# Two-layer attention with a recurrence: a projection one unit later, a later second load, and a reordered end

## The chip, the cores and the metric

The kernel runs on one core of a Trainium2 chip. The metric is the device time in microseconds (us), a median over runs. The engines are named as the profile names them: PE is TensorE, DVE is VectorE, ACT is ScalarE, POOL is GpSimd, SP is SyncE, which here only issues DMA transfers.

## The reference

The input is x of shape (4, 128, 64, 64), all fp32. Every image is taken as N = 4096 tokens of 128 channels. Layer 0 adds a full attention, layer 1 a causal one and then a recurrence:

```
x = x + conv_attention(groupnorm(x))     # q, k: 64 rows, v: 128; softmax over all 4096 keys
t = tokens(x)
t = t + causal_attention(layernorm(t))   # Wq, Wk, Wv: 128 x 128, scale 1/sqrt(128)
wx = batchnorm(layernorm(t) @ W)         # mean and variance over all 4 x 4096 tokens
y[k] = sigmoid(wx[k] + y[k-1] @ V.T)     # over the 4096 tokens of each image, y[-1] = 0
t = t + y
```

## The kernel before

**Units of attention.** For each image (batch b), each layer and each tile of QT = 512 queries (c from 0 to 7), the work is cut into units of two key blocks of 128. In layer 0 a tile has 16 units; in layer 1 it has only those up to the diagonal. A long loop over all units issues the scores of unit i (L1083 in layer 1, L1090 in layer 0), lets background work advance one step, and then issues the product of unit i-1 (L1134, which accumulates `av`). ScalarE turns scores into exponentials `s` (L1092, L1096), of which three buffers exist. VectorE adds them up in `total` (L1131).

**Background work.** It is written as generators. `step` advances every generator in `ends`, and the first ready one in `todo`, once for each unit. A `yield` in such a generator is thus a delay of one unit. The generators that matter here are:

- `gn_stats(b)`: statistics of image b by 8 `bn_stats` (L649), put in the list at the start of tile c = 2 of image 0 for the second image. They wait for the load of that image.
- `keys0(b, c)`: normalised tokens xg (L681), B0v added to X by POOL (L683), queries and keys pk (L686), the split of K into a high part (L707, L711) and a low part (L708), and the values pv (L715). For image 0 they are made during the first tile, one chunk of 512 keys (two units) after the other, as they are needed; those of the later images are made during layer 1 of the image before.
- `finish` (L942 to L966): the softmax sums, their reciprocals, and o = av / sum (L966).
- `project` (L971 to L985): in layer 1, it waits for some units, multiplies o by the value weights (po, L981), and adds the result to the residual as X2 (L984). The number of units waited for comes from the last line of `finish`.

A list scheduler then orders the instructions inside each engine, by its own costs and by what is ready. It may move an instruction far from its place in the program. Two stretches are kept in the order written: the first keys, and everything from `last_part` to `ordered.close()`.

**The loads of X.** `load_x(b)` issues 8 transfers of 256 KB on SP's queue (L508). With a second argument, POOL first copies a few columns of that argument over the target (L505), so that the transfers can't start before it. The second image is loaded this way, from `product` of unit 4 of the first tile.

**The last part.** The last tile is split in LAST = 384 queries and 128 queries. For the first 384, the product with the recurrence's weights is done early (`pw_early`), and only waits for their scales, which three matmuls spread over the partitions as a row (L917). ScalarE copies the row (L932), VectorE multiplies (L881, in `write_last`) and takes batch-norm statistics (L886). The same is done for the last 128 queries at the end (`raw_last`, L940). `scale` then merges all statistics to the gain and the bias of the batch norm.

**The recurrence.** The 4096 steps of an image are cut in chunks of CHUNK = (16, 16, 32, 32) steps, which all run side by side, each after WARM = 10 warm-up steps. Images 0, 1 and the pair (2, 3) form three chains. `first_step` is the first warm-up step, one sigmoid (L594), and for nearly all columns it uses a guessed scale before the true statistics are in. For the 15 columns of the last image that need the last queries (`BEHIND`), it is done afterwards with the true scale. `seed` puts gain times wx in PSUM (L1218), `advance` adds a matmul (L1233) and takes the sigmoid (L1234). Meanwhile VectorE adds finished steps to the residual (`residual`, L1258), in an order given by the list `late` with (image, first step, number of steps): 4 steps of a 32-step chunk are 512 elements a partition, 8 are 1024. When an image is complete, `store` sends its two halves (L1263). A check of the chunk boundaries (L1315 to L1328) follows, and its verdict decides on a branch to a slower general version.

Of the kernel before, what the change touches and what calls it, by code (L numbers as in the profile page):

```python
# [25 lines left out]
F32 = mybir.dt.float32  # L26
# [5 lines left out]
P = 128  # L32
QT = 512
# [431 lines left out]
CHUNK = (16, 16, 32, 32)  # L465
# [5 lines left out]
LAST = 384  # L471
# [3 lines left out]
def fast_kernel(  # L475
# [9 lines left out]
    nc = tc.nc  # L485
# [85 lines left out]
    def idle(ps, n):  # L571

        for _ in range(n):
            nc.tensor.matmul(ps, lhsT=nil, rhs=nil.unsqueeze(1).to_broadcast([P, QT // P, P]), start=True, stop=True)
# [14 lines left out]
    def first_step(b, at, n, scales):  # L589

        gain, bias = scales
        l = CHUNK[b] - WARM
        src = WX[b][:, l // 2, ds(at, n), l % 2]
        nc.scalar.activation(first[b][:, ds(at + 1, n)], src, AF.Sigmoid, scale=gain, bias=bias)  # L594

    with ExitStack() as actx:
# [10 lines left out]
        def misc(name):  # L607
            return ps_m.tile([P, QT], F32, tag="m", name=name)
# [269 lines left out]
        def write_last(off, w, row, pw):  # L878

            part = WX[B - 1][:, :, ds((N - QT + off) // CHUNK[-1], w // CHUNK[-1]), :]  # L880
            nc.vector.tensor_tensor(  # L881
                part.rearrange("p l s t -> p s l t"),
                *[t.rearrange("p (s l t) -> p s l t", l=CHUNK[-1] // 2, t=2) for t in (row, pw)], ALU.mult,
            )
            k = 9 if off else 3
            nc.vector.bn_stats(groups[:, k : k + 6], part)  # L886

        def last_part(av, pz, s):


            w, cols = P, ds(N - P, P)
            xt = X[B - 1][:, cols]
            wide = [ps_pair.tile([P, 2, QT], F32, tag="pair", name=f"last_{k}") for k in range(2)]
            avs = tmp.tile([P, QT], F32, tag="a", name="avs")[:, :w]
            nc.vector.tensor_copy(avs, av[:, :w])

            nc.scalar.activation(small.tile([P, 1], F32, name="sig"), s[:, 1, w - 1 : w], AF.Sigmoid)
            for b in range(2):
                first_step(b, 0, NC[b] - 1, scales["guess"])
            rz = small.tile([P, 1], F32, name="rz")  # L900
            nc.vector.reciprocal(rz, pz[:, 0:1])
            idle(misc("idle_last0"), 1)
            ptok = wide[0][:, 0, :w]
            nc.tensor.matmul(ptok, lhsT=avs, rhs=W1v, start=True, stop=True)
            prz = wide[1][:, 0, :w]
            nc.tensor.matmul(prz, lhsT=rz.to_broadcast([P, P]), rhs=ident, start=True, stop=True)
            po = misc("po_last")[:, :w]
            nc.tensor.matmul(po, lhsT=W1v, rhs=avs, start=True, stop=True)
            tok = scales["tok"]
            nc.vector.scalar_tensor_tensor(tok, ptok, rz, tok, ALU.mult, ALU.add)  # L910
            rzs = tmp.tile([P, QT], F32, tag="b", name="rzs")[:, :w]
            nc.scalar.copy(rzs, prz)

            pw_early, rstd_early = scales["early"]
            row = wide[1][:, 1, :LAST]
            for j in range(LAST // P):
                nc.tensor.matmul(  # L917
                    row[:, ts(j, P)], lhsT=rstd_early[:, j : j + 1].to_broadcast([P, P]), rhs=ident, start=True, stop=True
                )
            for b in range(2, B):  # L920
                first_step(b, 0, NC[b] - 1 - (BEHIND if b == B - 1 else 0), scales["guess"])
            stats = small.tile([P, 6], F32, name="lst_last")
            mv = small.tile([P, 2], F32, name="lmv_last")
            nc.vector.bn_stats(stats, tok)
            nc.vector.bn_aggr(mv, stats)
            rstd = small.tile([P, 1], F32, name="rstd_last")
            rsqrt(rstd, mv[:, 1:2], 1e-5, 1)
            nc.vector.scalar_tensor_tensor(rzs, rzs, GUARD, po, ALU.mult, ALU.mult)
            x2 = X2[B - 1][:, cols]
            nc.vector.scalar_tensor_tensor(x2, rzs, 1.0 / GUARD, xt, ALU.mult, ALU.add)  # L930
            rows = tmp.tile([P, QT], F32, tag="r", name="rows_early")[:, :LAST]
            nc.scalar.copy(rows, row)  # L932
            write_last(0, LAST, rows, pw_early)
            pw = misc("pw_last")[:, :w]
            nc.tensor.matmul(pw, lhsT=FWc, rhs=x2, start=True, stop=True)
            prow = wide[0][:, 1, :w]
            nc.tensor.matmul(prow, lhsT=rstd.to_broadcast([P, P]), rhs=ident, start=True, stop=True)
            idle(misc("idle_last2"), 2)
            raw = tmp.tile([P, QT], F32, tag="a", name="raw_last")[:, :w]
            nc.scalar.copy(raw, pw)  # L940
            write_last(LAST, w, raw, prow)
            scales["all"] = scale(mv, groups, "all")  # L942

        def finish(b, layer, c, off, w, av, total):

            name = f"{layer}_{b}_{c}_{off}"
            k = w // 32
            t = tmp.tile([P, QT], F32, tag="a", name=f"t_{name}")[:, :w]
            nc.vector.tensor_tensor(t, total[:, 0, :w], total[:, 1, :w], ALU.add)  # L949
            tt = tmp.tile([P, QT], F32, tag="b", name=f"tt_{name}")[:, :w]  # L950
            nc.vector.transpose(tt, t)  # L951
            part = small.tile([P, 16], F32, tag="part", name=f"part_{name}")
            nc.vector.tensor_reduce(part[:, :k], tt.rearrange("p (k j) -> p k j", j=32), AX.X, ALU.add)
            yield
            side = small.tile([32, 4, 16], F32, tag="side", name=f"side_{name}")
            for q in range(4):
                nc.vector.tensor_copy(side[:, q, :k], part[ds(32 * q, 32), :k])  # L957
            z = small.tile([P, 16], F32, tag="z", name=f"z_{name}")
            nc.vector.tensor_reduce(z[0:32, :k], side[:, :, :k].rearrange("j q k -> j k q"), AX.X, ALU.add)
            nc.vector.reciprocal(z[0:32, :k], z[0:32, :k])  # L960
            for q in range(1, 4):
                nc.vector.tensor_copy(z[ds(32 * q, 32), :k], z[0:32, :k])
            rb = tmp.tile([P, 16, 32], F32, tag="a", name=f"rb_{name}")[:, :k, :]
            nc.vector.transpose(rb, z[:, :k].unsqueeze(2).to_broadcast([P, k, 32]))  # L964
            o = tmp.tile([P, QT], F32, tag="b", name=f"o_{name}")[:, :w]
            nc.vector.scalar_tensor_tensor(  # L966
                o, rb.rearrange("p k j -> p (k j)"), GUARD, av[:, :w], ALU.mult, ALU.mult
            )
            yield from project(b, layer, c, off, w, o, 5 if w < QT else 3 if c == NQ - 1 else 2)

        def project(b, layer, c, off, w, o, waits):  # L971
            cols = ds(c * QT + off, w)
            xt = X[b][:, cols]
            if layer == 0:
                nc.vector.scalar_tensor_tensor(xt, o, 1.0 / GUARD, xt, ALU.mult, ALU.add)
                yield
                return
            for _ in range(waits):
                yield
            po = misc(f"po_{b}_{c}_{off}")[:, :w]  # L980
            nc.tensor.matmul(po, lhsT=W1v, rhs=o, start=True, stop=True)  # L981
            if c == 0:
                X2[b] = xpool.tile([P, N], F32, tag="X2", name=f"X2_{b}")
            nc.vector.scalar_tensor_tensor(X2[b][:, cols], po, 1.0 / GUARD, xt, ALU.mult, ALU.add)  # L984
            yield  # L985
# [119 lines left out]
        def product(i):  # L1105
# [8 lines left out]
            last = i == len(units) - 1  # L1114
            if last:

                pz = misc("pz_last")
                for h in range(2):
                    nc.tensor.matmul(pz[:, 0:1], lhsT=total[:, h, :w], rhs=ones[:, 0:1], start=h == 0, stop=False)
# [13 lines left out]
            for h in range(len(first)):  # L1133
# [1 line left out]
                    av[:, first[h] : w], lhsT=V[:, 2 * u + h, :], rhs=s[:, h, first[h] : w],  # L1135
                    start=u == 0 and h == 0, stop=2 * u + h == n - 1,
                )
            if (b, layer, c, u) == (0, 0, 0, 4):
                load_x(1, total[:, 0, 0:8])
            if last:  # L1140
                for h in range(2):
# [47 lines left out]
    with ExitStack() as fctx:  # L1189
# [76 lines left out]
        for k in range(2):  # L1266
            for g, group in enumerate(chains):
                ps = where[g, k] = ps_y.tile([P, 2, len(group), NC[group[0]]], F32, tag=f"y{g}", name=f"py{g}_{k}")
                idle(ps.rearrange("p t h s -> p (t h s)"), 1)
        seed(0, 0)  # L1270
        bias = shifted(gain, less, Fbeta, "all")
        seed(1, 0)
        seed(2, 0)
        bias0 = shifted(gain, less, Fb0, "all0")
        first_step(B - 1, NC[-1] - 1 - BEHIND, BEHIND, (gain, bias0))
        ordered.close()
        for k in range(1, 2):
            for g in range(3):
# [1 line left out]
        rest = ps_y.tile([P, QT], F32, tag="rest", name="rest", bufs=1)  # L1280
        late = [(1, l, 4) for l in range(0, CHUNK[1], 4)]
        late += [(b, l, 8) for l in range(0, CHUNK[2] - 8, 8) for b in (2, 3)]
        late += [(b, l, 4) for l in (CHUNK[2] - 8, CHUNK[2] - 4) for b in (2, 3)]
        for n in range(1, len(steps[2])):
            if n < last:
                for g in range(3):
# [91 lines left out]
```

## Time and profile before

| | before |
|---|---|
| device time, median of 3 | 2504.33 us (2504.14 to 2504.37) |
| profiled execution | 2503.85 us |
| its span | 2502.1 us |
| TensorE busy | 2466.4 us |
| VectorE busy | 1778.1 us |
| ScalarE busy | 1137.5 us |
| GpSimd busy | 206.9 us |
| DMA | 64.40 MB |

The span runs from the first to the last instruction in the profile. The profiled execution's own time is 1.75 us longer than its span. In the timeline each row gives the start, the duration, the engine, the line of the kernel, the operation and its operands; the brackets at the end say how long the engine was idle just before, and what released it. In the list of waits the numbers are the total in us, how many times, and the longest. Ends of matmuls are modelled, so a wait of TensorE read from them is approximate.

### The profile page before, as it was taken

How to read it: one execution, taken by the hardware profiler on the slowest of the kernel's cores; microseconds unless marked ns; L12 is line 12 of the kernel's file. 1: busy time of each engine (PE TensorE's matmuls, PEld its weight loads, DVE VectorE, ACT ScalarE, POOL GpSimd, SP SyncE). 2: the span in 40 equal slices, each digit the busy share in tenths (PEclk: the TensorE clock that was granted, in tenths of full speed). 3: DMA queues.
4: the chain of work that ended last, by engine and by line, in shares of the span. 5: the costliest groups of instructions: out<-in, count | busy, mean ns of one | idle time of the engine just before them, and what ended most of it. 6: DMA issues, size and time to landing. Idle time of an engine off the chain costs nothing.

```text
span 2502.1 us, 22482 instructions
## 1 busy us (share of the span) xinstructions
PE 2466.4 (99%) x7345; PEld 1339.4 (54%) x7345; DVE 1778.1 (71%) x3571; ACT 1137.5 (45%) x1422; POOL 206.9 (8%) x281
## 2 busy tenths in 40 slices
PE   7999999999999999999999999999999999999997
PEld 4555554444555555444555555544455555544465
DVE  7776669655977667856687676876578676786667
ACT  4444444454444444445444444454444444434456
POOL 2010001210000100110000010121010000010000
PEclk9999999999999999999999999999999999999999
DMA  2000001100100000100010000101010000010023
GB/s 75 9 17 9 17 9 41 27 17 13 51 13 9 17 9 18 39 25 13 22 46 13 13 9 18 34 26 26 13 47 17 9 14 12 9 34 17 9 74 138
DMA packets 154078, 64.40 MB, mean 26 GB/s; under 512 B 136160, under 2 KB 136928, under 8 KB 152160
## 3 DMA queue, kind: packets, MB, share of 16 engines
q1 hardware_dynamic: 151344, 59.27, 8.9%
q10 hardware_dynamic: 2608, 3.61, 0.4%
q8 instruction: 60, 0.98, 0.2%
q14 instruction: 66, 0.54, 0.1%
HBM read 31.66 MB, written 31.20 MB: 25 GB/s over the span
## 4 chain that ended last, share of the span: by engine, by line
PE 94%; DVE 3%; ACT 2%; issue 1%; POOL 0%; DVEq 0%; POOLq 0%; ACTq 0%
PE av L1134 52%; PE ps L1090 19%; PE ps L1083 17%; PE po L981 1%; PE pw_f L841 1%; PE pq L804 1%; PE pv L715 1%; PE pk L686 1%; ACT WX L1234 1%; DVE total L1131 1%; ACT states L1234 0%; PE pz L1233 0%; ACT WXp L1234 0%; ACT s L1092 0%; DVE stats L649 0%
## 5 line engine op out<-in xcount | busy, mean ns | idle before, releaser
L1131 DVE TENSOR_TENSOR total<-total,s 128x1024 f32<-128x1024 f32 (+5 forms) x809 | 882.5, 1094 | 539.6 <-ACT s L1092 290.9
L1134 PE MATMUL av<-s,WXp 128*128 128x512 f32 x2048 | 962.1, 592 | 0.0
L1092 ACT ACTIVATE s<-ps,shift 128x1024 f32<-128x1024 f32 x512 | 569.6, 1114 | 760.4 <-PE ps L1090 743.5
L1090 PE MATMUL ps<-q,K 128*128 128x512 f32 x2048 | 757.5, 492 | 1.7 <-DVE K L708 1.5
L1096 ACT ACTIVATE s<-ps,zero,R 128x512 f32<-128x512 f32 (+3 forms) x607 | 405.3, 718 | 513.6 <-PE ps L1083 506.5
L1134 PEld LDWEIGHTS av<-s,WXp 128*128 128x128 f32 x2048 | 384.7, 188 | 303.6 <-issue 263.1
L1090 PEld LDWEIGHTS ps<-q,K 128*128 128x128 f32 x2048 | 386.0, 189 | 290.4 <-issue 230.7
L1134 PE MATMUL av<-s,V 128*128 128x512 f32 (+3 forms) x1214 | 504.3, 538 | 0.0
L1083 PE MATMUL ps<-q,X 128*128 128x512 f32 (+3 forms) x1214 | 503.5, 537 | 0.0
L1083 PEld LDWEIGHTS ps<-q,X 128*128 128x128 f32 x1214 | 225.1, 190 | 236.1 <-issue 219.4
L1134 PEld LDWEIGHTS av<-s,V 128*128 128x128 f32 x1214 | 223.9, 190 | 229.2 <-issue 205.7
L579 POOL TENSOR_TENSOR rstd<-rstd,mhalf 128x4 f32<-128x4 f32 x32 | 32.4, 1011 | 1024.2 <-DVE rstd L578 1024.2
L1099 POOL TENSOR_SCALAR_AFFINE_SELECT s<-s 128x128 f32<-128x128 f32 x128 | 49.0, 387 | 532.8 <-ACT s L1096 531.7
L579 POOL TENSOR_TENSOR rstd_f<-rstd_f,mhalf 128x4 f32<-128x4 f32 (+1 forms) x32 | 47.3, 1480 | 383.1 <-DVE rstd_f L578 362.6
L683 POOL TENSOR_SCALAR X<-X,B0v 128x512 f32<-128x512 f32 x32 | 64.5, 2019 | 139.8 <-DVE xg L681 138.3
L796 DVE TENSOR_SCALAR V<-V,lmv,rstd 128x128 f32<-128x128 f32 x128 | 38.6, 344 | 37.0 <-POOL rstd L579 36.9
L729 DVE TENSOR_TENSOR q<-QR,qh 64x512 fp32r<-64x512 f32 x64 | 44.0, 688 | 6.8 <-PE ps L1090 5.5
L949 DVE TENSOR_TENSOR t<-total 128x512 f32<-128x512 f32 x64 | 44.0, 688 | 4.3 <-PE pfw L638 2.5
L951 DVE STREAM_TRANSPOSE tt<-t 128x512 f32<-128x512 f32 x64 | 45.2, 706 | 1.8
L964 DVE STREAM_TRANSPOSE rb<-z 128x512 f32<-128x512 f32 x64 | 44.8, 700 | 0.9
L966 DVE SCALAR_TENSOR_TENSOR o<-rb,av 128x512 f32<-128x512 f32 x64 | 43.6, 681 | 2.4
L957 DVE COPY side<-part 32x16 f32<-32x16 f32 (+1 forms) x256 | 41.3, 161 | 3.9
(191 smaller groups left out, 1227.8 us busy)
## 6 DMA issues: line engine op xcount, KB each, us to landing
turn<-t SPq DMA_DIRECT2D x32, 256.0 KB, 2.0
V<-turn SPq DMA_DIRECT2D x128, 64.0 KB, 2.5
turn_f<-t_f SPq DMA_DIRECT2D x31, 256.0 KB, 2.0
t_f<-turn_f SPq DMA_DIRECT2D x124, 64.0 KB, 2.5
X<-in_x SPq DMA_DIRECT2D x28, 256.0 KB, 4.5
kept<-X SPq DMA_DIRECT2D x24, 256.0 KB, 2.0
Y<-kept SPq DMA_DIRECT2D x6, 1024.0 KB, 8.3
out<-Y SPq DMA_DIRECT2D x5, 1024.0 KB, 6.0
```

The source lines that it names most:

```text
L579: nc.gpsimd.tensor_tensor(dst, dst, mhalf[:, :n], ALU.pow)
L683: nc.gpsimd.tensor_scalar(xt, xt, B0v, None, ALU.add)
L729: nc.vector.tensor_tensor(q[ds((1 - h) * CQ, CQ), h, :], src, high[rows, :], ALU.subtract)
L951: nc.vector.transpose(tt, t)
L964: nc.vector.transpose(rb, z[:, :k].unsqueeze(2).to_broadcast([P, k, 32]))
L1083: nc.tensor.matmul(ps[:, h, first[h] : w], lhsT=lhsT, rhs=q[:, off + first[h] : off + w], start=True, stop=True,)
L1090: nc.tensor.matmul(ps[:, h, :], lhsT=lhsT, rhs=q[:, k, :], start=k == 0, stop=k == 1)
L1092: nc.scalar.activation(s, ps, AF.Exp, bias=shift)
L1096: nc.scalar.activation(part, ps[:, h, first[h] : w], AF.Exp, scale=scale, bias=zero)
L1099: nc.gpsimd.affine_select(out=edge, in_=edge, pattern=[[1, P]], base=0, channel_multiplier=-1, compare_op=ALU.is_ge, fill=0.0,)
L1131: nc.vector.tensor_tensor(t, t, s[:, h, f:w], ALU.add)
L1134: nc.tensor.matmul(av[:, first[h] : w], lhsT=V[:, 2 * u + h, :], rhs=s[:, h, first[h] : w], start=u == 0 and h == 0, stop=2 * u + h == n - 1,)
```

## The change

It has six edits.

- The projection of tile c = 1 of layer 1 waits for 3 units instead of 2.
- The second image's load is placed behind unit 4 of the second tile instead of the first.
- The three matmuls of the row of the first 384 queries stand in `product`, ahead of the last unit's product. The copy of the row and the multiplication stand at the start of `last_part`. The statistics of that part come a little later, so `write_last` returns them as a function. A dummy matmul (`idle_last0`) is dropped.
- Of the guessed first steps, only image 0's stands ahead of the copy of `rzs`; those of images 1 to 3 come after it.
- The 15 late first steps and their bias stand behind the first seed, ahead of the general bias and the seeds of the other chains.
- The last residuals of images 2 and 3 are cut in pieces of 4, 2 and 2 steps instead of 4 and 4.

```diff
@@ write_last
             k = 9 if off else 3
-            nc.vector.bn_stats(groups[:, k : k + 6], part)
+            return lambda: nc.vector.bn_stats(groups[:, k : k + 6], part)
@@ last_part
+            pw_early, row = scales["early"]
+            rows = tmp.tile([P, QT], F32, tag="r", name="rows_early")[:, :LAST]
+            nc.scalar.copy(rows, row)
+            early_stats = write_last(0, LAST, rows, pw_early)
             avs = tmp.tile([P, QT], F32, tag="a", name="avs")[:, :w]
             nc.vector.tensor_copy(avs, av[:, :w])
             nc.scalar.activation(small.tile([P, 1], F32, name="sig"), s[:, 1, w - 1 : w], AF.Sigmoid)
-            for b in range(2):
-                first_step(b, 0, NC[b] - 1, scales["guess"])
+            first_step(0, 0, NC[0] - 1, scales["guess"])
             rz = small.tile([P, 1], F32, name="rz")
             nc.vector.reciprocal(rz, pz[:, 0:1])
-            idle(misc("idle_last0"), 1)
+            early_stats()
...
             nc.scalar.copy(rzs, prz)
-
-            pw_early, rstd_early = scales["early"]
-            row = wide[1][:, 1, :LAST]
-            for j in range(LAST // P):
-                nc.tensor.matmul(
-                    row[:, ts(j, P)], lhsT=rstd_early[:, j : j + 1].to_broadcast([P, P]), rhs=ident, start=True, stop=True
-                )
-            for b in range(2, B):
+            for b in range(1, B):
                 first_step(b, 0, NC[b] - 1 - (BEHIND if b == B - 1 else 0), scales["guess"])
...
-            rows = tmp.tile([P, QT], F32, tag="r", name="rows_early")[:, :LAST]
-            nc.scalar.copy(rows, row)
-            write_last(0, LAST, rows, pw_early)
...
-            write_last(LAST, w, raw, prow)
+            write_last(LAST, w, raw, prow)()
@@ finish
-            yield from project(b, layer, c, off, w, o, 5 if w < QT else 3 if c == NQ - 1 else 2)
+            yield from project(b, layer, c, off, w, o, 5 if w < QT else 3 if c in (1, NQ - 1) else 2)
@@ product, last unit
+                pw, rstd = scales["early"]
+                row = misc("row_early")[:, :LAST]
+                for j in range(LAST // P):
+                    nc.tensor.matmul(
+                        row[:, ts(j, P)], lhsT=rstd[:, j : j + 1].to_broadcast([P, P]), rhs=ident, start=True, stop=True
+                    )
+                scales["early"] = pw, row
...
-            if (b, layer, c, u) == (0, 0, 0, 4):
+            if (b, layer, c, u) == (0, 0, 1, 4):
                 load_x(1, total[:, 0, 0:8])
@@ behind the recurrence's first dummy matmuls
         seed(0, 0)
+        bias0 = shifted(gain, less, Fb0, "all0")
+        first_step(B - 1, NC[-1] - 1 - BEHIND, BEHIND, (gain, bias0))
         bias = shifted(gain, less, Fbeta, "all")
         seed(1, 0)
         seed(2, 0)
-        bias0 = shifted(gain, less, Fb0, "all0")
-        first_step(B - 1, NC[-1] - 1 - BEHIND, BEHIND, (gain, bias0))
         ordered.close()
...
-        late += [(b, l, 4) for l in (CHUNK[2] - 8, CHUNK[2] - 4) for b in (2, 3)]
+        late += [(b, CHUNK[2] - l, k) for l, k in ((8, 4), (4, 2), (2, 2)) for b in (2, 3)]
```

## The prediction

> **What bounds the kernel now.** I read the busy shares first, then the chain that ended last, TensorE's own waits, and the timeline around each wait that the change touches.
>
> ```profile
> span 2502.1 us, 22482 instructions
> PE 2466.4 (99%) x7345; PEld 1339.4 (54%) x7345; DVE 1778.1 (71%) x3571; ACT 1137.5 (45%) x1422; POOL 206.9 (8%) x281
> PE 94%; DVE 3%; ACT 2%; issue 1%; POOL 0%; DVEq 0%; POOLq 0%; ACTq 0%
> ```
>
> TensorE works 2466.4 of 2502.1 us, so an edit pays only where TensorE stands still inside the attention (to 2426 us), or in the end, where other engines set the pace. TensorE's waits give the price list:
>
> ```profile
> PE po L981 <- DVE o L966: 2.2, 3, 0.7
> PE ps L1090 <- DVE K L708: 1.5, 3, 0.6
> PE py L1233 <- ACT states L594: 0.4, 1, 0.4
> ```
>
> Three waits at po, three at layer 0's split key K, one at the 15 early first steps. By windows, TensorE is busy 54.46 of 56 us in 14 to 70, 9.71 of 12 in 2426 to 2438 (the last part), 46.85 of 49 in the recurrence, and 0.58 of 15 after 2487, when only stores run (DMA share 0.70).
>
> [...]
>
> **1. The po of tile c=1 waits a third unit.** Timeline of batch 0:
>
> ```profile
> 408.14 0.69 DVE L966 SCALAR_TENSOR_TENSOR o<-rb,av 128x512 f32<-128x512 f32 x1
> 408.88 1.12 PE L981 MATMUL po<-o,W1v 128*128 128x512 f32 x2 [0.74 <-DVE o L966]
> ```
>
> TensorE reaches po before DVE ends o (408.83). The idle shown is 0.74, but matmul ends are modelled; against the 0.43 us pace of 512-column passes, starts slip by 0.91, and the next matmul starts at 409.84, 0.96 after po, where two passes take 0.86: 1.0 us lost. It recurs at 1010.43 and 1611.99, so batches 0 to 2. In batch 3, which makes no next keys, o is 3.27 us early: nothing. In the order of instructions after the change, one value product (pv, 0.86), one unit's av (1.72) and the next score's (0.64) come ahead of po, 3.2 us of work that is ready: po is reached at 411.2 at the earliest, o is done at 408.83. o's buffer is held a unit longer; the next tile's finish wants it some six units on. What is late next: X2 (L984), 3.2 us later, is not read for units; POOL's select of a diagonal tile, behind the X add (L683), would be ready at about 415.1, its av due at 416.1; the exp behind the K copies keeps some 0.2 of its 0.36 us. **-3.0.**
>
> **2. The second load (batch 1's X) is issued one tile later.** It starts when POOL's marker (35.35) lets SP issue; 8 bn_stats of X are then placed among tile 0's key work:
>
> ```profile
> 46.46 1.23 DVE L1131 TENSOR_TENSOR total<-total,s 128x1024 f32<-128x1024 f32 x1
> 47.72 0.69 DVE L708 TENSOR_TENSOR K<-k,kh 64x512 fp32r<-64x512 f32 x1
> 48.55 0.93 PE L1090 MATMUL ps<-q,K 128*128 128x512 f32 x3 [0.59 <-DVE K L708]
> 48.90 0.69 DVE L649 BATCH_NORM_STATS2 stats<-X 128x6 f32<-128x512 f32 x1
> ```
>
> The starts of pk are 7.30, 7.87, 7.54 and 7.04 apart, where the same passes need 7.01; with 0.4 behind the last, 2.1 us are lost. After, no stats lie here, but the order also splits an av around the score, so TensorE arrives earlier and waits some 0.33 for K in each chunk. Stepped through with the trace's durations, pk comes at 42.73, 50.07, 57.41, 64.75 (before 42.61, 50.48, 58.02, 65.06) and the last score at 69.91 instead of 70.55: **-0.6**, bounds 0 and -1.7. In tile 1 the 8 stats (8 x 0.65 by their pitch, 5.2 us) follow five totals; a unit of 2.645 us keeps DVE 1.23, so 1.4 are free in each, and three s buffers cover the rest. What moves is POOL's marker (0.20, nothing urgent behind it on POOL) and SP's 8 issues with their 2 MB; on SP the turn of tile 0's result now stands near them, and its reader is the layer-1 values, tiles away: nothing.
>
> **3. Last part: row of 384 ahead.** Before:
>
> ```profile
> 2430.45 0.48 ACT L932 COPY rows_early<-last 128x384 f32<-128x384 f32 x1 [0.24 <-PE last L917]
> 2430.96 0.56 DVE L881 TENSOR_TENSOR WXp<-rows_early,pw_f 128x384 f32<-128x384 f32 x1 [0.45 <-ACT rows_early L932]
> 2431.55 0.56 DVE L886 BATCH_NORM_STATS2 groups<-WXp 128x6 f32<-128x384 f32 x1
> 2432.03 0.27 DVE L881 TENSOR_TENSOR WXp<-raw_last,last 128x128 f32<-128x128 f32 x1
> ```
>
> The early product and its statistics (two times 0.56) hold DVE until 2432.03, though raw_last is there at 2431.35. After: the three row matmuls run at about 2426.2; the copy ends at 2427.57, the table load moves from 2426.76 to 2427.59 (+0.83), the first steps of chain 0 and rzs follow by 2429.7, the other first steps end at 2431.02, still ahead of raw. On DVE the early product (0.56) and statistics (0.56) fall in 2427.6 to 2429.1, delaying ptok and X2 by 0.1; raw_last ends 2431.45 and the last product starts 2431.47 instead of 2432.03: **-0.56**. Bounds: the 0.1 and the later first steps could cost 0.4 of it; dropping idle_last0 removes 0.22 of dummy work in a stage whose clock stood at 1.00.
>
> **4. The 15 first steps ahead of the seeds' bias.** Before:
>
> ```profile
> 2435.32 0.47 ACT L1234 ACTIVATE states<-py,bias_all 128x255 f32<-128x255 f32 x1 [3.97 <-PE py L1233]
> 2435.70 0.39 ACT L594 ACTIVATE states<-WXp,bias_all,gain_all 128x15 f32<-128x15 f32 x1
> 2435.99 0.46 ACT L1234 ACTIVATE states<-py,bias_all 128x255 f32<-128x255 f32 x1
> 2436.13 0.48 PE L1233 MATMUL py<-states,FV 128*128 128x254 f32 x1 [0.38 <-ACT states L594]
> ```
>
> ScalarE idles 3.97 us, then runs L594 between chains 0 and 1, and chain 2's matmul waits for it. After, L594 (0.39) lies in that idle time, 0.64 behind the first seed; bias and seeds 1 and 2 come 0.13 later, hidden. Counted from the first seed, ScalarE's steady pitch of 0.43 begins at 4.10 instead of 4.56: **-0.46**, bounds 0 and -0.6.
>
> **5. Late residuals in smaller pieces.**
>
> ```profile
> 2486.03 0.69 DVE L1258 TENSOR_TENSOR Y<-Y,WXp 128x512 f32<-128x512 f32 x1 [0.19 <-ACT WXp L1234]
> 2486.64 0.69 DVE L1258 TENSOR_TENSOR X<-X,WXp 128x512 f32<-128x512 f32 x1
> 2487.35 0.33 SPq L1263 DMA_DIRECT2D out<-X  x1
> ```
>
> DVE is busy without a break from 2474. A residual of 512 has a pitch of 0.60, one of 256 (0.42) an estimated 0.335. Four of 256 follow X's piece of 2485.14: Y 2485.74, X 2486.08, and for the last two steps, which are in by then, Y 2486.41 and X 2486.75. Y's store is issued at 2486.87 (+0.12), X's at 2487.21 (-0.14). The end is set by 4.2 MB draining at over 400 GB/s to about 2499.3, which starts with Y: **+0.1**, bounds -0.15 and +0.2.
>
> **Sum:** -3.0 -0.6 -0.56 -0.46 +0.1 = -4.5 us. The profiled execution took 2503.85 (span 2502.1 and 1.75 around it) and becomes 2499.3; the median shown, 2504.33, stands 0.48 above it, hence **2499.8**. A measurement of this kernel tells about 0.2%, 5.0 us, from no change: the bound is 2499.3, and the forecast lies just inside it.
>
> **The rivals.**
> - *The head gives back all 2.1* (for it: it is lost now; against it: K is still last in the worked order), 1.5 more: 2498.3. Chance 0.14.
> - *Half of po's gain turns into another wait*, in the exp behind the K copies with 0.36 of slack or at the select behind L683: 3 x 0.5 lost: 2501.3. Chance 0.18.
> - *The edits of the ends do nothing*, because the stores drain to the same moment: parts 3 to 5 give 0, 2504.33-3.6=2500.7. Against it: the drain starts with the last residual. Chance 0.05.
> - *Slower: DVE parks on batch 1's statistics in tile 1.* DVE works in order; if the first X piece lands L after its turn, totals stop and exps run out of s buffers: 3 x 2.645 = 7.9 less a unit in work is 5.3 us of slack. The loss is L-5.3, beating the 4.5 gained from L=9.8, and past 0.2% above before from 14.8; at 16 it gives 2499.8+10.7=2510.5. Against it: the first piece needed at most 3.6 us (issue 35.58, stats 39.13). Chance 0.05.
>
> **How the numbers follow.** The forecast has 0.58, its own range 2498.9 to 2500.8, of which 0.20 lies beyond 0.2%. Faster: 0.20+0.14=0.34; slower 0.05; the rest, 0.61, within. The range 2497.8 to 2502.6 takes in the first three rivals with their bounds, and leaves the parked DVE out.
>
> **What would show it.** Right: no po wait of 0.7 in TensorE's list; no L649 before 70 us; rows_early at about 2427.1, the first seed 0.56 closer to the last exp; L594 ahead of the first states of L1234; four last residuals of 256. Wrong: an idle DVE in front of L649 in tile 1, a new TensorE wait near 415 us or its repeats, K waits above 0.33, or a change of the span that these places do not hold.

## The result, and the profile after

| | before | changed |
|---|---|---|
| device time, median of 20 runs each | 2504.70 us (2503.66 to 2505.83) | 2500.03 us (2499.37 to 2501.83) |
| ratio | | 0.9981, 95% interval 0.9976 to 0.9987 |
| profiled execution, its span | 2503.85, 2502.1 us | 2499.56, 2497.8 us |

The kernel is 4.7 us faster by the medians, 4.3 us by the profiled executions. The forecast of 2499.8 us lies 0.2 us from the median. Some of its terms were wrong all the same, so this nearness is in part luck, and the rest of the study is about those terms.

The page of the changed kernel, first the span, then the busy shares, then the chain that ended last:

```profile
span 2497.8 us, 22485 instructions
PE 2465.7 (99%) x7344; PEld 1337.9 (54%) x7344; DVE 1777.1 (71%) x3573; ACT 1137.8 (46%) x1422; POOL 211.3 (8%) x281
PE 96%; ACT 1%; DVE 1%; issue 1%; POOL 0%; DVEq 0%; POOLq 0%; ACTq 0%
```

TensorE's work is the same within 1 us; its share of the chain rose from 94% to 96%. What went away is standing still. TensorE's list of waits in the changed kernel (total, times, longest) shows where:

```profile
PE pw_last L928 <- DVE X L926: 1.3, 1, 1.3
PE ps L1083 <- DVE K L708: 0.6, 3, 0.2
PE py L1234 <- DVE py L1219: 0.4, 1, 0.4
```

The wait at po is gone. The wait for K is smaller, and it is not gone. The new wait of 1.3 at pw_last is the place where the row matmuls stood before; the chain of the last part ran through VectorE there already.

To see where the time came from, I cut each profiled execution at the starts of five instructions that every kernel here has: the first pk matmul, the first score of unit 20 (in the second tile), the last score, the first seed of the recurrence on VectorE, and the last sigmoid. The stretches between them, in us:

| stretch | before | changed | difference | forecast |
|---|---|---|---|---|
| start to first pk | 14.02 | 14.01 | 0.0 | 0 |
| first pk to unit 20 (the first tile) | 71.42 | 71.21 | -0.21 | -0.6 |
| unit 20 to the last score | 2340.19 | 2337.17 | -3.02 | -3.0 |
| last score to the first seed (last part) | 8.37 | 7.82 | -0.55 | -0.56 |
| first seed to the last sigmoid | 51.89 | 51.63 | -0.26 | -0.46 |
| last sigmoid to the end | 16.23 | 15.99 | -0.24 | +0.1 |
| sum | 2502.12 | 2497.83 | -4.29 | -4.5 |

**po.** The timeline of the changed kernel around po of image 0. The columns are start, duration, engine, line, operation, operands and count:

```profile
407.76 1.05 PE L715 MATMUL pv<-W0v,xg 128*128 128x128 f32 x8
407.93 0.69 DVE L959 SCALAR_TENSOR_TENSOR o<-rb,av 128x512 f32<-128x512 f32 x1
408.66 1.88 PE L1135 MATMUL av<-s,V 128*128 128x512 f32 x4
411.03 1.02 PE L974 MATMUL po<-o,W1v 128*128 128x512 f32 x2
```

While VectorE computes o (until 408.62), TensorE works on pv and av without a bracket of idle time in front of any row. It reaches po at 411.03, 2.4 us after o is ready.

**The last part.** The same rows as those shown before the change:

```profile
2423.87 0.48 ACT L896 COPY rows_early<-row_early 128x384 f32<-128x384 f32 x1 [0.35 <-PE row_early L1113]
2424.38 0.56 DVE L881 TENSOR_TENSOR WXp<-rows_early,pw_f 128x384 f32<-128x384 f32 x1 [1.30 <-ACT rows_early L896]
2425.19 0.54 DVE L886 BATCH_NORM_STATS2 groups<-WXp 128x6 f32<-128x384 f32 x1
2427.92 0.27 ACT L933 COPY raw_last<-pw_last 128x128 f32<-128x128 f32 x1
2428.22 0.29 DVE L881 TENSOR_TENSOR WXp<-raw_last,last 128x128 f32<-128x128 f32 x1 [0.88 <-ACT raw_last L933]
```

The product of the first 384 queries now runs before VectorE has the last av, and its statistics run in a gap just behind. When raw_last comes, VectorE has been idle for 0.88 us and starts at once. Before, it started 0.7 us after raw_last had come. ScalarE's ACT_TABLE_LOAD took 1.28 us in both kernels, from 2426.76 before and from 2424.36 in the changed one, and the activation behind it started 0.02 us after its end (2428.06 and 2425.66).

### The profile page after: what moved, and what is told of

It is laid out like the page before. It is cut to its first block, busy times and chain, and to the rows that moved or that the text cites. A ratio compares the mean times of both kernels' runs of the same rounds, so it can differ in the third digit from the quotient of the medians.

```text
span 2497.8 us, 22485 instructions
## 1 busy us (share of the span) xinstructions
PE 2465.7 (99%) x7344; PEld 1337.9 (54%) x7344; DVE 1777.1 (71%) x3573; ACT 1137.8 (46%) x1422; POOL 211.3 (8%) x281
## 4 chain that ended last, share of the span: by engine, by line
PE 96%; ACT 1%; DVE 1%; issue 1%; POOL 0%; DVEq 0%; POOLq 0%; ACTq 0%
PE av L1135 53%; PE ps L1083 19%; PE ps L1076 18%; PE pq L804 1%; PE po L974 1%; PE pk L686 1%; PE pv L715 1%; PE pw_f L841 1%; ACT WX L1235 1%; ACT states L1235 0%; ACT WXp L1235 0%; DVE Y L1259 0%; PE py L1234 0%; DVE X L1259 0%; DVE total L1132 0%
```

## The experiments

Where no ratio is given, the kernel ran once. Those single times, 2499.68 to 2500.37 us, lie within the range of the changed kernel, so only their marks are read. The runs fall in several series, and the kernel before took 2504.12 to 2504.48 us in them, so a ratio is always to the kernel before of the same series. The cuts of code leave out lines that stay as they are.

### The later po alone

```diff
 # the kernel before
-... 3 if c == NQ - 1 else 2)
+... 3 if c in (1, NQ - 1) else 2)
```

> The kernel before with only the later po of layer 1's tile c=1 (three units instead of two). Theory A, three equal stalls behind o: the last scores of the attention come 3.0 us earlier than in the kernel before (1.0 behind each of the three po), the list of waits of TensorE no longer has po, and the time is 3.0 us below before, ratio 0.9988. Rival, half of it comes back as a wait behind the K copies or the select: 1.5 us earlier, and a new slip of 0.5 us shortly after 415, 1017 and 1619 us.

Measured: 2501.29 us against 2504.48 before, ratio 0.9987 (0.9981 to 0.9994). From unit 20 to the last score it took 2337.17 us, 3.02 less than before and exactly what the changed kernel takes. po is no longer in TensorE's list of waits, and no new slip follows 415, 1017 or 1619 us. Three stalls of 1.0 us are the whole of this part, and nothing of it came back elsewhere.

### The load back in the first tile

```diff
 # the changed kernel
-            if (b, layer, c, u) == (0, 0, 1, 4):
+            if (b, layer, c, u) == (0, 0, 0, 4):
```

> The changed kernel with the second load put back into the first tile. The two profiles show that the later load moved the start of the second tile by 0.2 us only. Theory B, the low part of K stands behind a total and the query copy on VectorE with or without the statistics: the last scores of tile 0 come back to 70.55 us, all later marks 0.2 us later than in the changed kernel, and the three K waits of 0.5 to 0.6 return. Rival, the scheduler's other split of av is what costs: the marks of this kernel are at or below those of the changed kernel.

Measured: the first tile took 71.46 us instead of 71.21. In TensorE's list, the waits for K are again three of up to 0.6:

```profile
PE ps L1083 <- DVE K L708: 1.1, 3, 0.6
```

So the later load is worth 0.25 us here, and the statistics are only a small part of what makes K late. Behind unit 20 the load costs nothing at its new place: that stretch is 2337.17 us with either.

### The queries of image 0 on ScalarE

```diff
 # the changed kernel, keys0
-                if b:
+                if b or c:
                     nc.scalar.activation(rows, pk[low, :], AF.Identity, bias=B0qk[low, :])
```

> The changed kernel, in which the queries of image 0 (but for the first chunk) are read from PSUM by ScalarE, as those of the other images are, instead of by VectorE. Theory B, VectorE's order in front of K (total 1.22, query copy 0.74, high part 0.42, low part 0.69) sets the pitch of 7.49 us of the four chunks after 35 us: with 0.74 less there, TensorE doesn't wait, the pitch is 7.01, the second tile starts 1.9 us earlier, and the time is 1.9 below the changed kernel (about 6.5 below before, ratio 0.9974). Rival, the pitch is set by ScalarE or by TensorE's own order: it stays at 7.4 to 7.5 and the time at that of the changed kernel.

Measured: 2499.83 us, ratio to before 0.9982 (0.9975 to 0.9989). The first tile took 71.41 us, no better than before the change, and the pitch of pk (the time from the start of one chunk to the next) was 7.61. The theory as priced fell. Rows from the timeline of this kernel show why:

```profile
50.22 1.02 PE L686 MATMUL pk<-xg,W0qk 128*128 128x512 f32 x2
51.08 1.88 PE L1135 MATMUL av<-s,WXp 128*128 128x512 f32 x4
52.80 1.05 PE L715 MATMUL pv<-W0v,xg 128*128 128x128 f32 x8
53.34 0.69 DVE L708 TENSOR_TENSOR K<-k,kh 64x512 fp32r<-64x512 f32 x1
54.18 0.70 PE L1083 MATMUL ps<-q,K 128*128 128x512 f32 x2 [0.33 <-DVE K L708]
```

K is done 3.81 us after pk starts, as intended: in the changed kernel it takes 4.55. But TensorE's order moved with it. The scheduler no longer puts half an av (0.86) between pv and the score. TensorE now has pk, av and pv to do before the score, 0.86 + 1.72 + 0.86 = 3.44 us, and it is again too early. In the changed kernel that half av stands at 61.12:

```profile
57.65 1.02 PE L686 MATMUL pk<-xg,W0qk 128*128 128x512 f32 x2
58.51 1.88 PE L1135 MATMUL av<-s,WXp 128*128 128x512 f32 x4
59.05 1.22 DVE L1132 TENSOR_TENSOR total<-total,s 128x1024 f32<-128x1024 f32 x1 [0.61 <-ACT s L1085]
60.23 1.05 PE L715 MATMUL pv<-W0v,xg 128*128 128x128 f32 x8
60.29 0.74 DVE L697 TENSOR_SCALAR QR<-pk,B0qk 64x512 f32<-64x512 f32 x1
61.05 0.42 DVE L707 TENSOR_SCALAR kh<-k 64x512 int32<-64x512 int32 x1
61.12 1.02 PE L1135 MATMUL av<-s,WXp 128*128 128x512 f32 x2
61.51 0.69 DVE L708 TENSOR_TENSOR K<-k,kh 64x512 fp32r<-64x512 f32 x1
62.35 0.70 PE L1083 MATMUL ps<-q,K 128*128 128x512 f32 x2 [0.21 <-DVE K L708]
```

VectorE has no statistics to take here. Its total waits for the exponential, and the query copy and the two halves of K follow it. TensorE has 4.3 us of work for a chain of 4.55.

### Key chunks one unit earlier

This run tests the theory that the last one led to: what counts is the latency from pk to K against TensorE's work in between.

```diff
 # the changed kernel, score
-            if (b, layer, c) == (0, 0, 0) and u % 2 == 0:
-                whole(("k0", 0, u // 2))
+            if (b, layer, c) == (0, 0, 0) and (u == 0 or u % 2 and (u + 1) // 2 < NQ):
+                whole(("k0", 0, (u + 1) // 2))
```

> The changed kernel, in which tile 0's key chunks are finished one unit earlier. The run with the queries on ScalarE showed K 0.7 us earlier and TensorE's order changed with it, so that the pitch stayed. Theory E, the pitch of the chunks is the latency from pk to K (3.8 to 4.6 us) against the work that TensorE has between pk and the score that reads K: here that work is two units' av, pv and a score of the older chunk (about 6 us). Then no K wait is left, the pitch is 7.01, the second tile starts 1.9 us earlier, and the time is 1.9 below the changed kernel. Rival, VectorE and ScalarE together can't keep 7.01 in these chunks: the pitch stays over 7.3 and exp waits show instead.

Measured: 2498.44 us, ratio to before 0.9977 (0.9969 to 0.9986). The chunks start at 39.49, 46.53, 53.57 and 60.61, a pitch of 7.04, and the first tile took 69.08 us, 2.1 less than in the changed kernel. K no longer appears in TensorE's list of waits. The timeline around the last chunk:

```profile
60.61 1.02 PE L686 MATMUL pk<-xg,W0qk 128*128 128x512 f32 x2
63.99 1.18 PE L1083 MATMUL ps<-q,K 128*128 128x512 f32 x4
64.92 0.69 DVE L708 TENSOR_TENSOR K<-k,kh 64x512 fp32r<-64x512 f32 x1
65.00 1.88 PE L1135 MATMUL av<-s,WXp 128*128 128x512 f32 x4
66.32 0.79 PE L1083 MATMUL ps<-q,K 128*128 128x512 f32 x1
```

K takes 5.0 us from pk here, longer than ever, and nobody waits for it, because the score at 63.99 reads the older chunk and an av follows. The theory holds, and its rival, that VectorE and ScalarE can't keep the pace, does not.

The profiled execution became 1.2 us shorter than that of the changed kernel, not 2.1. The last part took 8.17 us instead of 7.82, and the end 16.55 instead of 15.99. The first of these is a gap on VectorE in front of the first seed:

```profile
2427.79 0.16 DVE L855 TENSOR_TENSOR gain_all<-gain_all,Fgamma 128x1 f32<-128x1 f32 x1 [0.60 <-POOL gain_all L579]
2428.41 0.49 DVE L1219 TENSOR_SCALAR py<-WX,gain_all 128x255 f32<-128x255 f32 x1 [0.46 <-PE py L574]
```

In the changed kernel the seed starts 0.27 after gain_all, here 0.62. The profile names the dummy matmuls, but the last of the six, by its modelled end, was over at 2428.12. What held the seed for the remaining 0.3 us stays open. It isn't the gain: in the two kernels below that have a seed on ScalarE too, ScalarE's seed starts 0.28 us behind gain_all, and VectorE's first one 0.62.

### The 15 first steps back behind the seeds

```diff
 # the changed kernel
         seed(0, 0)
-        bias0 = shifted(gain, less, Fb0, "all0")
-        first_step(B - 1, NC[-1] - 1 - BEHIND, BEHIND, (gain, bias0))
         bias = shifted(gain, less, Fbeta, "all")
         seed(1, 0)
         seed(2, 0)
+        bias0 = shifted(gain, less, Fb0, "all0")
+        first_step(B - 1, NC[-1] - 1 - BEHIND, BEHIND, (gain, bias0))
```

> The changed kernel with the 15 late first steps and their bias behind the seeds of the other chains again. Theory D, their move is worth 0.28 us and nothing else: from the last scores to the first seed it is 7.8 us as in the changed kernel (8.4 before), the steady pitch of ScalarE's sigmoids begins 4.56 us behind that seed instead of 4.28, and the last sigmoid is 0.3 us later. Rival, the row of 384 and the first steps are what freed it: 4.28 as in the changed kernel.

Measured: the last part took 7.82 us as in the changed kernel, the steady pitch began 4.56 us behind the first seed, and the recurrence took 51.93 us instead of 51.63. So the late first steps are worth 0.3 and do nothing for the last part. Its 0.55 belongs to the other edits there together: the row, the order of the guessed first steps and the dropped dummy matmul, which no run separates.

### One seed on ScalarE

The forecast had 0.46 for the first steps. The changed kernel's timeline shows the missing part:

```profile
2431.25 0.48 DVE L1219 TENSOR_SCALAR py<-WXp,gain_all 128x254 f32<-128x254 f32 x1
2431.64 1.39 DVE L1219 TENSOR_SCALAR py<-WX,gain_all 128x510 f32<-128x510 f32 x2
2432.94 0.74 DVE L1219 TENSOR_SCALAR py<-WXp,gain_all 128x508 f32<-128x508 f32 x1
```

The three seeds of the second round start at 2431.64, about 2432.29 and 2432.94, at a pitch of 0.65. The third starts 2.7 us behind the first seed, as in the kernel before: the edit did not move it. The sigmoids of that round follow at 3.02, 3.67 and 4.28 behind the first seed, at VectorE's pitch and not at ScalarE's 0.43.

```diff
 # the kernel with key chunks one unit earlier
+            dst = ...  # the seed's target and source, as before
+            wx = ...
-            nc.vector.tensor_scalar(...)
+            if (g, k) == (2, 0):
+                nc.scalar.activation(dst, wx, AF.Copy, scale=gain)
+            else:
+                nc.vector.tensor_scalar(dst, wx, gain, None, ALU.mult)
...
         seed(0, 0)
+        seed(2, 0)
         bias0 = shifted(gain, less, Fb0, "all0")
...
         seed(1, 0)
-        seed(2, 0)
```

> The kernel with key chunks one unit earlier, and besides the first seed of the pair (2, 3) is written by ScalarE, which is idle then. Theory D, the recurrence's second round is set by VectorE's seeds at a pitch of 0.65, which start 0.39 later for each seed ahead of them: the second round begins 0.39 earlier, the steady pitch begins about 3.9 us behind the first seed instead of 4.28, and the last sigmoid is 0.4 us earlier. Rival, the loop of matmul and sigmoid sets the second round: it stays at 4.28, or later, since ScalarE has the seed to write.

Measured: 2498.16 us, ratio to before 0.9975 (0.9966 to 0.9985). The sixth sigmoid, at which the steady pitch began at 4.28 in the changed kernel, comes 3.95 us behind VectorE's first seed, and the recurrence takes 51.28 us, 0.33 less than without this edit (51.61). VectorE's seeds set the second round. This version is 6.3 us faster than the kernel before in its series; the changed kernel was 4.7 us faster in its own.

### The tail: pieces of 4 and 4, pieces of 8, and again

```diff
 # the changed kernel: first variant, second variant
-        late += [(b, CHUNK[2] - l, k) for l, k in ((8, 4), (4, 2), (2, 2)) for b in (2, 3)]
+        late += [(b, l, 4) for l in (CHUNK[2] - 8, CHUNK[2] - 4) for b in (2, 3)]
+        late += [(b, CHUNK[2] - 8, 8) for b in (2, 3)]
```

> The changed kernel with the last residuals in two pieces of 4 steps again, for each of the images 2 and 3. Theory C, the end is set by 4.2 MB of stores that start with the first of the two stores: the first store is issued 0.11 us earlier than in the changed kernel and the second 0.08 later, and the end, counted from the last sigmoid, is the same within 0.1 us. Rival, the second store's issue sets the end: counted from the last sigmoid the end is 0.1 to 0.3 us later.

> The changed kernel with the last residuals of images 2 and 3 in one piece of 8 steps each. Both can only start behind the last sigmoid, so the first store is issued about 0.7 us later than in the changed kernel, counted from the last sigmoid, and the second 1.4 later. Theory C, the first store's issue sets the end: the end, counted from the last sigmoid, is 0.7 us later. Rival, the second store's issue sets it: 1.4 us later. Third, the drain varies by more than either: no relation.

Measured: with pieces of 4 and 4, the first store was issued 0.09 us earlier and the second 0.09 later (SyncE's halves, counted from the last sigmoid), where the forecast's working had 0.12 and 0.14. The end came 16.19 us behind the last sigmoid, against 15.99 for the changed kernel. With one piece of 8, the first store was 0.44 later, the second 1.15 later, and the end came at 16.64. The last two residuals of the changed kernel and its first store, for comparison:

```profile
2482.34 0.42 DVE L1259 TENSOR_TENSOR Y<-Y,WXp 128x256 f32<-128x256 f32 x1
2482.68 0.42 DVE L1259 TENSOR_TENSOR X<-X,WXp 128x256 f32<-128x256 f32 x1
2482.79 0.33 SPq L1264 DMA_DIRECT2D out<-Y  x1
```

These ends would fit a tail worth 0.2 us, if other profiles with the same pieces of 4, 2 and 2 did not end at 16.5 (16.53 with the load back, 16.55 and 16.54 with the earlier chunks). So I ran the changed kernel again, and put the pieces of 4 and 4 in the best version.

> The changed kernel as it is, once more, for the end. Of the six profiles whose late residuals are cut in pieces of 4, 2 and 2 steps, three end 16.0 us behind the last sigmoid and three 16.5. Theory F, the drain of the last stores differs from one execution to the next: this one shows 16.0 or 16.5, while every mark ahead of the stores agrees with the first profile within 0.1 us. Rival, it belongs to the kernel: 15.99 again.

> The kernel with key chunks one unit earlier and one seed on ScalarE, with the late residuals in pieces of 4 and 4 steps as before the change. Theory F: the pieces don't decide the end; the time is that of the same kernel with pieces of 4, 2 and 2 (2498.2) within 0.5 us, and from the last sigmoid to the end it is 16.2 us. Rival, the smaller pieces are worth 0.2 us or more: 2498.4 to 2498.8.

Measured: the changed kernel again ended 16.07 us behind the last sigmoid. The best version with pieces of 4 and 4 took 2497.97 us, ratio to before 0.9975 (0.9964 to 0.9985), with an end of 16.21; with pieces of 4, 2 and 2 it took 2498.16, in a series whose kernel before was 0.31 slower. Over all profiles, pieces of 4, 2 and 2 end at 15.98 to 16.07 in five and at 16.48 to 16.55 in four; pieces of 4 and 4 end at 16.19 to 16.23 in all four.

The traces show where the two groups part. Each image is stored in two halves, one issued by SyncE and one by ScalarE, on two DMA queues. The profile's line for the last store, in the changed kernel, with the load back, and with one piece of 8 (its size, and the us from issue to landing):

```profile
out<-X ACTq DMA_DIRECT2D x1, 1024.0 KB, 13.0
out<-X ACTq DMA_DIRECT2D x1, 1024.0 KB, 13.5
out<-X ACTq DMA_DIRECT2D x1, 1024.0 KB, 11.2
```

The end follows the last landing by 1.59 us in every profile but that with one piece of 8. In the five with the early end, the first packet on ScalarE's queue starts 0.62 us behind the first on SyncE's, and the last store lands at 14.39 to 14.48. In the four with the late end the distance is 0.31, and the last store lands at 14.89 to 14.97. With pieces of 4 and 4 the distance is 0.62 in all four, and the last store lands at 14.61 to 14.65. Against these, the smaller pieces end about 0.2 us earlier where the queues start 0.62 apart, and 0.3 later where they start 0.31 apart. What sets the distance is not shown. It may belong to the kernel: the only one profiled twice kept it, and of the 23 executions of the two kernels with earlier chunks and the late end none was more than 0.1 us below its profiled one. On average the split has no gain that these runs can see.

The run with one piece of 8 doesn't test what its forecast asked. Its stores were issued later and yet the last one landed earlier than in any other profile, at 13.7. What came last there was TensorE's part of the branch on the verdict of the check: it took 6.6 us and ended at 15.25 (14.5 to 14.7 in the other profiles, whose last landing came at about the same time or later). In these runs a later first store thus did not mean a later landing.

### A fourth unit, and a still later load

```diff
 # the changed kernel: two separate runs
-... 3 if c in (1, NQ - 1) else 2)
+... 4 if c == 1 else 3 if c == NQ - 1 else 2)

-            if (b, layer, c, u) == (0, 0, 1, 4):
+            if (b, layer, c, u) == (0, 0, 1, 6):
```

> The changed kernel with four units of wait for po of tile c=1 instead of three. Theory A, o is ready 2.2 us before po is reached already, so a fourth unit gives nothing: the stretch from tile 1 of image 0 to the last scores is as long as in the changed kernel (2337.17 us), within 0.1. Rival, po or what waits for X2 is short of slack in some batch: longer by 0.3 or more.

> The changed kernel with the second load issued two units later still (5.3 us). The first two statistics of image 1 then stand ahead of the total of unit 24 on VectorE, with the load issued at about 95.2 us and landing about 2.6 us behind its issue, as in the changed kernel. Price of the slower rival: a wait of VectorE for the load of less than 5.3 us costs TensorE nothing. So VectorE shows a wait of 0 to 2 us in front of the statistics, and the stretch from tile 1 to the last scores stays at 2337.2 us. Against it: each us of VectorE's wait lengthens that stretch by as much.

Measured: with four units, the stretch from unit 20 to the last score is 2337.18 us; the third unit had taken all there was, and the fourth costs nothing. With the load two units later, VectorE did park on the statistics:

```profile
95.85 1.23 DVE L1132 TENSOR_TENSOR total<-total,s 128x1024 f32<-128x1024 f32 x1 [0.65 <-ACT s L1085]
98.78 1.48 DVE L649 BATCH_NORM_STATS2 stats<-X 128x6 f32<-128x512 f32 x2 [1.71 <-DMA X<-in_x]
100.17 2.54 DVE L1132 TENSOR_TENSOR total<-total,s 128x1024 f32<-128x1024 f32 x2
```

It stood still for 1.71 us, and the stretch stayed at 2337.17 us. This is the slower rival's parked VectorE, with a wait below the 5.3 us of slack that the prediction estimated, and it costs nothing, as priced. The total that stands behind the statistics in VectorE's order started only at 100.17. A wait above 5.3 us was not tried. In the changed kernel the first piece landed at 92.56 us and its statistics started at 93.32, so nothing waited. The whole times of these two single runs, 2500.29 and 2500.03 us, are at the changed kernel's, with 0.2 to 0.4 us more in the last part in both (8.06 and 8.22). Their traces show the cause: the granted TensorE clock was 0.5 of full speed for 3.4 us there, from 2427.6 and from 2427.5, while it was 1.00 in the last part of all other profiles. The two matmuls that spread the last scale then took 0.63 us instead of 0.39, and VectorE's last product had to wait for them (first row: changed kernel; the others: four units):

```profile
2427.72 0.39 PE L930 MATMUL last<-ident,rstd_last 128*128 128x128 f32 x2
2427.65 0.63 PE L930 MATMUL last<-ident,rstd_last 128*128 128x128 f32 x2
2428.39 0.29 DVE L881 TENSOR_TENSOR WXp<-raw_last,last 128x128 f32<-128x128 f32 x1 [1.12 <-PE last L930]
```

## Why the prediction was right, and where its steps were off

- **po, -3.0: right in place and size.** 3.02 in the changed kernel and in the run with this edit alone. The rival in which half comes back did not happen: the stretch did not change by 0.05 us between any two kernels with three or four units.
- **The second load, -0.6: mis-sized, -0.21.** The failed term is "waits some 0.33 for K in each chunk". Stepped with the trace's durations, the pitch of pk came out at 7.34 for the last three chunks; it is 7.48 to 7.49 against 7.01, so 0.47 is lost in each (0.37 in the chunk before). The list of waits gives these as 0.2 each, since ends of matmuls are modelled; the starts show the loss. The step took the statistics out of VectorE's queue, but came out with K too early. The timeline shows the total ahead of K waiting 0.6 us for the exponential of the same unit; which link the step had too short is not on record. The rival that would have given back all 2.1 us failed too: K was still the last to come, as the prediction said against it. The runs show that the loss is real and that its cover is the distance between pk and its score: one unit more gave 2.1 us.
- **The row of 384, -0.56: right in the changed kernel**, 0.55. raw_last came 0.07 later, counted from the last score, where 0.10 was worked out, and the later first steps were hidden as worked out. But the same code gave only 0.15 to 0.3 in five other kernels (8.06 to 8.22 instead of 7.82). In two of these five the clock fell to 0.5. The prediction had named the dropped dummy matmul as a risk to the clock. Whether it, or the new gap of 1.3 in front of pw_last, brought the fall on is not shown: ten of the twelve profiles with the new order kept 1.00, as did the two with the old one.
- **The first steps, -0.46: mis-sized, -0.26** in the changed kernel and 0.3 when undone. The term that failed is the start of the steady pitch at 4.10 behind the first seed: it is 4.28, because the third seed of the second round runs at VectorE's pitch of 0.65 too. Taking one seed off VectorE moved it to 3.95.
- **The residuals, +0.1: the issue times moved the right way** (first store later by 0.09, second earlier by 0.09), the end was not settled. The profile shows -0.24; the other profiles with the same pieces put it between -0.25 and +0.32. The price of a cut held: in the changed kernel the four pieces of 256 start at 2481.67, 2482.01, 2482.34 and 2482.68, 0.34 us apart (0.335 was estimated), and the piece of 512 ahead of them keeps VectorE for 0.60, from 2481.07, so a piece cut in two takes some 0.08 us more. The premise that the end is set by a drain that starts with Y's store is not borne out: with one piece of 8 that store was issued 0.44 later and the last landing came 0.7 earlier. (The prediction also says that VectorE is busy without a break from 2474; its own line at 2486.03 shows a break of 0.19, which its sum does not use.)
- **The sum, -4.5 against -4.29** by the profiled executions. Two gains that were too large by 0.4 and 0.2 stood against an end that was 0.3 better, and that end is the one of two values that happened to help. The total is closer than its parts.
- The rival in which the ends do nothing because the stores drain to the same moment is refuted for the changed kernel: the last part and the recurrence became 0.81 shorter, and the stretch behind the last sigmoid did not grow in its two profiles (15.99 and 16.07, against 16.23).

## What to carry to other kernels

When an engine waits for the last link of a chain, compare the whole latency of the chain with the work that stands between its first and its last link on the waiting engine. Here the chain took 4.55 us and the work 4.3. Shortening a link failed (the first tile took 71.41 us instead of 71.21), because the scheduler took work out of that gap at the same time; making the gap longer by a whole unit of work succeeded (69.08 us). A wait that recurs the same way in each batch can be priced from one occurrence, by the slip of the starts against the undisturbed pace, and multiplied: po cost 1.0 us in image 0, and the later po gave 3.02 in three images.

## What was not expected

- In kernels that were changed far from it, the first seed of the recurrence was late by 0.35 us in three of them (8.17 us instead of 7.82), with the reason open. In two others the last part took 8.06 and 8.22, with the granted clock at 0.5 for 3.4 us of it.
- The last store landed 14.4 or 14.9 us behind the last sigmoid with the same store code, according to whether the two queues began 0.62 or 0.31 us apart. A difference of 0.5 us is as large as what the edit of the last part gave.
- Two runs with one profile each differed by 0.5 us before the first matmul (14.02 and 14.54 us in the kernel before and in the one with only the later po, which are equal there). A single span must be read from a mark, not from zero.
